# Context keys and values by seven block products: block sums made in DRAM, combined weights beside the first output projection

## The chip, the cores and the metric

The kernel runs on one core of one Trainium2 chip. The metric is device time in microseconds (us) of one execution. Engines are named as in the profile: PE is TensorE (PEld its weight loads), DVE is VectorE, ACT is ScalarE, POOL is GpSimd and SP is SyncE, which here issues DMAs alone.

## What is computed

A post-norm decoder layer on 8 batches of 100 tokens, width 1024, with a context of 8 x 722 tokens. All in float32:

```
x = layernorm(x + retention(x))                 # 8 heads, Wq Wk Wv Wg Wo
x = layernorm(x + cross_attention(x, context))  # 16 query heads, 4 key/value heads of 128
x = layernorm(x + ffn(x))                       # silu(x Wgate) * (x Wup), then Wdown

# cross attention, per batch:
k_ctx = rms_norm(context @ wk_ctx)   # 722 x (4 heads x 128)
v_ctx = context @ wv_ctx             # 722 x (4 heads x 128)
k, v  = own keys (normed, rotated) and own values, joined behind k_ctx, v_ctx
out   = softmax(q k' / sqrt(128) + causal mask) v @ wo
```

The change concerns `k_ctx` and `v_ctx`. For one batch and one key/value head, both are products of a 1024 x 128 weight with the same 722 x 1024 context.

## The kernel before

Activations stand transposed: the feature on the partitions, tokens along the free axis. A float32 operand is kept as two float32r parts, high and low: `split` and `split2` (line 68) make the high part with a copy on ACT and the low part with a subtraction on DVE. `mm3` (lines 90, 93, 94) multiplies high by high, high by low and low by high, so that one block product of 128 features costs three matmuls.

The program is recorded once in Python; a scheduler then orders each engine's instructions by its own estimate of times, and each engine works through its list in that order. A semaphore wait at the head of a list holds everything behind it, on SP's list of DMA issues too.

The stages, in order of time:

- **Retention** (to about 440 us). Heads 1 to 7 use `seven`, which makes a 2 x 2 block product with seven block products for eight. At the end of `core`, once for each of the eight context weights, the weight is split and stored in DRAM (`wcd`), with an accumulating DMA issued by POOL (line 566).
- **First output projection and norm** (`out_proj`, to about 600 us). Weights come through `load_w`: a DMA into one of three staging buffers `wst`, then the split.
- **Cross-attention queries, keys and values of the own tokens** (to about 830 us). Each of 40 projections is followed by a sum over the partitions on POOL (`all_red`, line 141), which the norm on ACT and DVE waits for. The first context batch is loaded and the keys of its first two heads are made here.
- **Context attention** (830 to 1606 us): a loop over 8 batches `b` and 4 key/value heads `kv`. At each batch `load_context` brings in the context of the batch in eight pieces `cs` of 128 x 724 or 128 x 720 and splits each into four `big` tiles. For each head, `context_keys` makes the keys as two column halves of 362 and 360 tokens, 24 matmuls each (`proj`), evacuates them from PSUM (lines 705 to 708) and has POOL sum their squares (line 706, tile `kss`). That sum goes through DRAM (`row`, `rr`) to become a column of scales. `context_values` makes the values in the same way (line 719). Then come the scores (seven chunks, 21 matmuls), a maximum over the partitions on POOL (`mb<-mx`), exponentials, the split of the probabilities into `ph` and `pl`, a sum on POOL (`mb<-sm`) and the product with the values (21 matmuls). The result `oh` goes to DRAM (`o2d`).
- **Second output projection** and the **feed-forward part** with `seven` (1606 us to the end).

Context weights and activations are held so:

- `load_ws` loads one split weight (1 MB) into one of four `w` slots; a head uses two.
- The tiles `big` have four slots, all four used by one batch's context.
- Keys (`kall`) and queries (`q`) have two slots each.

Of the kernel before, what the change touches and what calls it, by code (L numbers as in the profile page):

```python
# [8 lines left out]
F32 = mybir.dt.float32  # L9
# [7 lines left out]
P = 128  # L17
B, T, D = 8, 100, 1024
NB = 4
# [3 lines left out]
SC, SH = 722, 362  # L23
SN = [SH, SC - SH]
# [16 lines left out]
def decoder_layer(ctx, tc, xT, cT, w1, wo1, w2, wo2, wc, w3, wd, gw, qw, kw, trig, dec, mask, out):  # L41
# [44 lines left out]

    pin = tc.keep_in_program_order

# [66 lines left out]

    def tokens_first(pool, acc, copied=True, bufs=1, got=None):
# [17 lines left out]
    o2d = dr.tile([B, P, NKV, 4, 2, T], FR, name="o2d")  # L174
    zd = dr.tile([2, P, KT, N], F32, name="zd")
    zd2 = dr.tile([2, P, KT, N], F32, name="zd2")
    wcd = dr.tile([2 * NKV, P, 2, KT * P], FR, name="wcd")
    hd = dr.tile([QT - 1, 7, P, 2, QT, N], FR, name="hd")
# [35 lines left out]
    kws = cp.tile([P, 1], F32, name="kws")  # L214
# [3 lines left out]
    def load_constants(p, trg):  # L218
# [8 lines left out]
        nc.vector.tensor_scalar(kws, wts[:, 3:4], -0.5 * math.sqrt(P), None, ALU.mult)  # L227
        nc.vector.tensor_scalar(tq, trg[:, 2:4], wts[:, 2:3], None, ALU.mult)
# [9 lines left out]
    def out_proj(half, w, load_o, res, yp, ybufs, p, make_z, dst, z, steps={}, home=None):  # L238
# [7 lines left out]
        for ms in [range(first)] + [[m] for m in range(first, KT)]:  # L246
# [4 lines left out]
            for c in range(2):  # L251
                for m, acc in zip(ms, accs):
                    wt = load_w(w[m, c])
                    for k in range(KT):
# [124 lines left out]

    H = QT * P  # L380
# [96 lines left out]
    with sbuf("l1", 2) as p:  # L477
# [48 lines left out]

        HB = ((0, 0), (1, 1), (0, 1), (1, 0))
# [84 lines left out]
        def after_qk(h, c):  # L612
            for (half, i), acc in c:
                of_qk(half, i, acc)

        def after_v(h, c):
            for (half, blk), acc in c:
                of_v(half, blk, acc, (half, blk) == HB[3])
            core(h)

        def after_g(h, c):
            gated(h, {hb: silu(acc, None if hb == HB[3] else acc) for hb, acc in c})

# [23 lines left out]
    with sbuf("ln1", 1) as p:  # L647
        z1, todo = [], {}
        for half in range(2):
            todo, _ = out_proj(half, wo1, load_o1, xT, p, 2, p, lambda _: [  # L650
                z1p.tile([P, 2, QT, N], FR, tag="z", name="z") for _ in range(2)], zd, z1, todo)
# [13 lines left out]
    kapool = sbuf("ka", 2, "right")  # L665
    ka = kapool.__enter__()
    cz = []
# [21 lines left out]
    def load_context(b):  # L689
        for _ in context_steps(b, wp, 3):  # L690
            pass

    def context_keys(kv):

        kall = ka.tile([P, 2, SC + T], FR, tag="kall", name="kall")
# [17 lines left out]
    def context_values(kv):  # L713

        wv = load_ws(2 * kv + 1)
        vt = ka.tile([P, SC], F32, bufs=1, tag="cvt", name="cvt")
# [12 lines left out]
    with sbuf("l2", 2) as p:  # L729
        ctx0 = context_steps(0, p, 2, behind)  # L730
        for g, group in enumerate(groups):
# [3 lines left out]
            if g in (1, 5):  # L735
                step, kept = context_keys(len(early))
                early.append(kept)
            for half in range(g == 0, 2):
                bs = slice(half * NB, (half + 1) * NB)
                for (kv, i), w in zip(group, ws):  # L740
# [4 lines left out]
                    unit += 1  # L745
                    if i == 5:
# [523 lines left out]
```

## Time and profile before

| | |
|---|---|
| three timed runs | 2483.72, 2486.41, 2486.9 us; median 2486.41 us |
| span of the profiled execution, first to last instruction | 2480.1 us |
| granted TensorE clock | 0.999 |
| PE busy / PEld busy | 2456.9 us / 2436.3 us |
| DVE busy | 1950.7 us |
| ACT busy | 1341.0 us |
| POOL busy | 481.8 us |
| moved by DMA | 433.98 MB, 175 GB/s over the span |

The profile holds one execution. The times of the runs include what lies around the span; for the median that is 6.3 us. An engine's busy time is the union of its instructions. A printed duration runs to an instruction's end, and a next one may start before that end, so sums of durations can exceed the busy time.

### The profile page before, as it was taken

What the parts mean: (1) busy time and instruction counts of PE and PEld (TensorE: products, weight loads), DVE (VectorE), ACT (ScalarE), POOL (GpSimd) and SP (SyncE); (2) the same over time, 40 slices, a digit from 0 to 9 for tenths busy, and PEclk for the clock granted to TensorE, in tenths of its full rate; (3) what the DMA queues carried; (4) which work ended last, traced back from release to release, by engine and by line L of the source; (5) the groups of instructions that cost most, each with busy time, mean ns of one, the idle gap of its engine ahead of it and who ended that gap; (6) DMA issues with size and microseconds to landing.
All of it is one profiled execution on the core that took longest, in us unless ns stands there. A gap on an engine that the chain in (4) does not pass through costs nothing.

```text
span 2480.1 us, 37239 instructions
## 1 busy us (share of the span) xinstructions
PE 2456.9 (99%) x14068; PEld 2436.3 (98%) x14068; DVE 1950.7 (79%) x3101; ACT 1341.0 (54%) x2258; POOL 481.8 (19%) x266
## 2 busy tenths in 40 slices
PE   9999999999999999999999999999999999999997
PEld 9999999999999999999999999999999999999997
DVE  7777877556898798998998999757987777666756
ACT  6667676334888565665566666524544454432221
POOL 0111111100566343443443443100000000000000
PEclk9999999999999999999999999999999999999999
DMA  7333345775544555455455454465455444389731
GB/s 244 112 112 129 132 142 186 242 257 182 173 163 144 196 185 175 130 180 165 154 181 156 155 187 170 156 241 172 160 176 189 161 161 161 122 303 325 265 103 54
DMA packets 221891, 433.98 MB, mean 175 GB/s; under 512 B 47338, under 2 KB 163946, under 8 KB 209294
## 3 DMA queue, kind: packets, MB, share of 16 engines
q1 hardware_dynamic: 217358, 419.49, 50.2%
q0 software_dynamic: 3200, 10.75, 1.9%
q8 instruction: 111, 1.82, 0.3%
q10 hardware_dynamic: 1152, 1.34, 0.2%
q14 instruction: 70, 0.57, 0.1%
HBM read 322.18 MB, written 109.35 MB: 174 GB/s over the span
## 4 chain that ended last, share of the span: by engine, by line
PE 94%; DVE 2%; DMA 2%; ACT 1%; issue 1%; SPq 0%; DVEq 0%; ACTq 0%
PE a L94 20%; PE a L93 20%; PE a L90 20%; PE s L94 9%; PE s L93 9%; PE s L90 9%; PE v L93 2%; PE v L94 2%; PE v L90 2%; PE s L554 1%; PE s L795 1%; PE s L166 1%; DVE y L331 0%; PE v L546 0%; DMA wst<-in_w 0%
## 5 line engine op out<-in xcount | busy, mean ns | idle before, releaser
L90 PE MATMUL a<-big,w 128*128 128x400 f32 (+2 forms) x1808 | 610.7, 339 | 2.0 <-DVE z L270 0.7
L93 PE MATMUL a<-big,w 128*128 128x400 f32 (+2 forms) x1808 | 610.0, 337 | 0.5 <-DVE big L68 0.5
L94 PE MATMUL a<-big,w 128*128 128x400 f32 (+2 forms) x1808 | 608.5, 337 | 0.5 <-DVE w L68 0.5
L68 ACT CAST w<-wst 128x1024 fp32r<-128x1024 f32 (+1 forms) x231 | 239.5, 1039 | 380.3 <-PE s L94 147.6
L68 DVE TENSOR_TENSOR w<-wst,w 128x1024 fp32r<-128x1024 f32 (+1 forms) x231 | 281.1, 1217 | 132.5 <-ACT w L68 130.6
L90 PEld LDWEIGHTS a<-big,w 128*128 128x128 f32 x1808 | 340.2, 188 | 4.5 <-ACT big L68 1.1
L93 PEld LDWEIGHTS a<-big,w 128*128 128x128 f32 x1808 | 340.9, 189 | 2.5 <-DVE big L68 1.3
L94 PEld LDWEIGHTS a<-big,w 128*128 128x128 f32 x1808 | 340.8, 189 | 1.4 <-DVE w L68 0.8
L90 PE MATMUL a<-z,w 128*128 128x400 f32 x680 | 235.0, 346 | 0.4 <-ACT w L68 0.4
L93 PE MATMUL a<-z,w 128*128 128x400 f32 x680 | 235.1, 346 | 0.0
L94 PE MATMUL a<-z,w 128*128 128x400 f32 x680 | 234.9, 346 | 0.0
L90 PE MATMUL s<-big,w 128*128 128x400 f32 x664 | 230.3, 347 | 0.5 <-DMA big<-o2d 0.4
L94 PE MATMUL s<-big,w 128*128 128x400 f32 x664 | 229.2, 346 | 0.4 <-DVE w L68 0.4
L93 PE MATMUL s<-big,w 128*128 128x400 f32 x664 | 229.5, 346 | 0.0
L706 POOL PARTITION_ALL_REDUCE kss<-ksq x64 | 170.2, 2659 | 113.4 <-ACT ksq L705 112.6
L141 POOL PARTITION_ALL_REDUCE ss<-sq x56 | 148.4, 2651 | 199.3 <-ACT sq L750 110.1
L830 ACT ACTIVATE s<-s,rk 128x400 f32<-128x400 f32 x160 | 88.1, 591 | 90.9 <-DVE sm L850 65.3
L90 PEld LDWEIGHTS a<-z,w 128*128 128x128 f32 x680 | 127.8, 188 | 1.2 <-ACT w L68 0.8
L94 PEld LDWEIGHTS a<-z,w 128*128 128x128 f32 x680 | 128.7, 189 | 0.0
L93 PEld LDWEIGHTS a<-z,w 128*128 128x128 f32 x680 | 127.8, 188 | 0.4
L90 PEld LDWEIGHTS s<-big,w 128*128 128x128 f32 x664 | 124.8, 188 | 2.1 <-issue 0.7
L94 PEld LDWEIGHTS s<-big,w 128*128 128x128 f32 x664 | 125.4, 189 | 0.7 <-DVE w L68 0.7
(366 smaller groups left out, 5462.3 us busy)
## 6 DMA issues: line engine op xcount, KB each, us to landing
wst<-in_w SPq DMA_DIRECT2D x135, 512.0 KB
w<-wcd SPq DMA_DIRECT2D x64, 1024.0 KB
wst<-in_wo SPq DMA_DIRECT2D x64, 512.0 KB
hd<-h SPq DMA_DIRECT2D x12, 1400.0 KB
wst<-in_wd SPq DMA_DIRECT2D x64, 256.0 KB
big<-o1d SPq DMA_DIRECT2D x16, 800.0 KB
qd<-d SPq DMA_DIRECT2D x32, 400.0 KB
q<-qd SPq DMA_DIRECT2D x32, 400.0 KB
```

What stands on the lines that cost most here:

```text
L68: return nc.scalar.copy(hi, src), nc.vector.tensor_tensor(lo, src, f32(hi), ALU.subtract)
L90: i = nc.tensor.matmul(acc, lh, rh, start=start, stop=False, skip_group_check=chain)
L93: nc.tensor.matmul(acc, lh, rl, start=False, stop=False, skip_group_check=chain)
L94: nc.tensor.matmul(acc, ll, rh, start=False, stop=stop, skip_group_check=chain)
L141: nc.gpsimd.partition_all_reduce(y, x, P, op)
L166: nc.tensor.transpose(tr[0:T, b * P:(b + 1) * P], vt[:, b * T:(b + 1) * T], ident)
L554: nc.tensor.matmul(bt(o)[:, b], vv[:, b * P:(b + 1) * P], pf[:, b], start=True, stop=True)
L706: nc.gpsimd.partition_all_reduce(ss[:, at], sq[:, at], P, RED.add)
L795: nc.tensor.transpose(tr[0:rows, (c - c0) * P:(c - c0 + 1) * P], vt[:, c * P:c * P + rows], ident)
L830: nc.scalar.activation(sc, sp, AF.Copy, scale=rk[:, c:c + 1])
```

## The change

From the second batch on, keys and values of one head come from one 2 x 2 block product. The context of a batch is cut into four blocks: features 0 to 511 and 512 to 1023, tokens 0 to 361 and 360 to 721 (two tokens are in both). The weights are cut into feature halves: values and keys. Seven block products of 4 x 3 matmuls with 362 columns take the place of eight.

- **Sums of context blocks.** Four for each batch, made in DRAM: `block_sums` copies four blocks into `td` with DMAs issued by SP, and adds to them with four accumulating DMAs issued by POOL. It is a generator, advanced three times per head in the retention stage and then at every third projection of the own queries.
- **Combined weights.** `context_weights` loads both plain context weights of a head, forms four combinations with four DVE operations, splits them (ACT and DVE) and stores them in `wcx`. It is advanced at the weight loads of `out_proj` of the first output projection, from the 13th on.
- **`load_context`** loads and splits seven operands (three blocks as they are, four sums) in 14 pieces of 128 x 724, into the four `big` slots and three new `op` slots.
- **`load_pair`** loads 3.5 MB of weights for a head into the four `w` slots, for 2 MB before.
- **`context_pair`** makes the seven products and puts the keys together in `ks`, the values in `vt`, in SBUF: some parts are copied from PSUM by ACT, others added by DVE. Keys are then scaled, split and squared from `ks`.
- **Room in SBUF.** `kall` has one slot in `ka`, and one more (`ke`) during the first batch; `q` and others in `cx` have one. The score tiles lose the unused part of their first chunk. The pool `y2` of the second output projection opens after the context stage and not before it. `ofs` is dropped, and `oh` is stored with high and low parts apart.

```diff
+    def load_pair(kv):
+        plain = load_ws(2 * kv + 1)
+        ws = [plain[:, :, :H], plain[:, :, H:]]
+        for j, n in ((0, 2), (2, 1), (3, 1)):
+            w = wp.tile([P, 2, 2, H], FR, tag="w", name="w", bufs=4)
+            nc.sync.dma_start(out=f32(w[:, :n]), in_=f32(wcx[kv, :, j:j + n]))
+            ws += [w[:, i] for i in range(n)]
+            if j == 2:
+                nc.sync.dma_start(out=f32(w[:, 1]), in_=f32(wcd[2 * kv, :, :, H:]))
+                ws.append(w[:, 1])
+        return ws
+    def block(b, i, j):
+        return cT[b, :, i * QT:(i + 1) * QT, j * S0:j * S0 + SH]
+    def block_sums():
+        for b in range(1, B):
+            for i, src in enumerate(((0, 0), (1, 1), (0, 0), (1, 0))):
+                pin(nc.sync.dma_start(out=td[b - 1, i], in_=block(b, *src)))
+            yield
+            for i, src in enumerate((block(b, 0, 1), block(b, 0, 1), td[b - 1, 1], td[b - 1, 2])):
+                pin(nc.gpsimd.dma_start(out=td[b - 1, i], in_=src, accum_op=ALU.add))
+                if i > 0:
+                    yield
...
+    def context_weights(pool):
+        for _ in range(12):
+            yield
+        for kv in range(NKV):
+            r0, r1 = (pool.tile([P, KT * P], F32, tag=t, name=t) for t in ("wv", "wk"))
+            nc.sync.dma_start(out=r0, in_=wc[2 * kv + 1])
+            nc.sync.dma_start(out=r1, in_=wc[2 * kv])
...
+            v.tensor_tensor(a22, a22, a21, ALU.subtract)
+            v.tensor_tensor(a21, a11, a21, ALU.subtract)
+            v.scalar_tensor_tensor(a11, a22, -1.0, a11, ALU.mult, ALU.subtract)
+            v.scalar_tensor_tensor(a12, a12, -1.0, a11, ALU.mult, ALU.subtract)
+            for j, srcs in ((0, (a11, a21)), (2, (a22, a12))):
...
+                for n, src in enumerate(srcs):
+                    split2(w[:, n, 0], w[:, n, 1], src)
+                nc.sync.dma_start(out=f32(wcx[kv, :, j:j + 2]), in_=f32(w))
+                for _ in range(2):
+                    yield
...
-    def load_context(b):
-        for _ in context_steps(b, wp, 3):
-            pass
+    def load_context(b, pool):
+        ops = []
+        for src in (block(b, 0, 0), block(b, 1, 0), td[b - 1, 2], td[b - 1, 1], td[b - 1, 0], td[b - 1, 3], block(b, 1, 1)):
+            t = big([P, 2, QT, SH]) if len(ops) < 4 else pool.tile([P, 2, QT, SH], FR, tag="op", name="op", bufs=3)
+            for k in range(0, QT, 2):
...
+                nc.sync.dma_start(out=cs, in_=src[:, k:k + 2])
+                split(t[:, :, k:k + 2], cs)
+            ops.append(t)
+        return ops
...
+    def context_pair(kv, ops, pool):
...
+        def keys(part, scale):
+            nc.scalar.activation(kall[:, 0, part], ks[:, part], AF.Copy, scale=scale)
+            nc.vector.scalar_tensor_tensor(
+                kall[:, 1, part], ks[:, part], scale, f32(kall[:, 0, part]), ALU.mult, ALU.subtract)
+            nc.scalar.activation(ks[:, part], ks[:, part], AF.Square)
+            nc.gpsimd.partition_all_reduce(ss[:, part], ks[:, part], P, RED.add)
+        add = nc.vector.tensor_tensor
+        prod(x, 0)
+        now(nc.scalar.copy, vt[:, lo], x)
+        prod(z, 1)
+        now(add, vt[:, lo], z, vt[:, lo], ALU.add)
+        prod(x, 2, False)
+        now(nc.scalar.copy, ks[:, lo], x)
+        prod(y, 3)
+        now(nc.scalar.copy, ks[:, hi], y[:, at])
+        prod(x, 4, False)
+        now(add, ks[:, hi], x[:, at], ks[:, hi], ALU.add)
+        keys(hi, kwn)
+        prod(y, 5, False)
+        now(add, ks[:, lo], y, ks[:, lo], ALU.add)
+        keys(lo, kws)
+        nc.sync.dma_start(out=row.rearrange("c p -> (c p)")[None, :], in_=ss[0:1])
+        prod(x, 6, False)
+        nc.scalar.activation(vt[:, hi], x[:, at], AF.Copy, scale=-1.0)
+        return (kall, row), vt
```

## The prediction, before the changed kernel was run

> **What bounds the kernel now.** I read the page's busy row first, then the windows by stage, then the groups and waits of the context stage, then timelines of one batch.
>
> ```profile
> PE 2456.9 (99%) x14068; PEld 2436.3 (98%) x14068; DVE 1950.7 (79%) x3101; ACT 1341.0 (54%) x2258; POOL 481.8 (19%) x266
> ```
>
> By this row TensorE is the bound, and work taken from it should be time. The windows (stretch, its length, then busy us of PE, PEld, DVE, ACT, POOL, clock, DMA share, GB/s) say how close the second engine is:
>
> ```profile
> 500.00:640.00 140.00, 140.00 (x776) 137.78 (x775) 91.58 (x141) 63.92 (x103) 12.43 (x13) 1.00 0.64 219
> 640.00:830.00 190.00, 190.00 (x1065) 189.91 (x1065) 165.16 (x301) 148.13 (x294) 109.85 (x47) 1.00 0.51 173
> ...
> 1125.00:1225.00 100.00, 100.00 (x610) 99.30 (x609) 91.76 (x163) 61.37 (x120) 40.25 (x22) 1.00 0.53 162
> 1225.00:1325.00 100.00, 100.00 (x606) 99.41 (x606) 92.97 (x159) 62.67 (x119) 39.40 (x22) 1.00 0.53 169
> ```
>
> In the context stage, where nearly all of the change lies, DVE is busy 92% beside a full PE. The length of a batch there is read off SP's timeline, at the first context load of two batches:
>
> ```profile
> 969.38 1.20 SPq L678 DMA_DIRECT2D cs<-in_cT  x2
> ...
> 1064.42 1.20 SPq L678 DMA_DIRECT2D cs<-in_cT  x2
> ```
>
> A batch takes 95.05 us. Over five batches (1014.5 to 1489.8 us) DVE is busy 438.2 us: 87.6 in a batch, idle 7.4.
>
> **PE, removed.** Per batch and head, 96 projection matmuls become 84. One takes, from start to start in PE's timeline:
>
> ```profile
> 1060.28 0.33 PE L93 MATMUL a<-big,w 128*128 128x362 f32 x1
> ...
> 1067.56 0.33 PE L90 MATMUL a<-big,w 128*128 128x362 f32 x1
> ```
>
> These are 44 matmuls apart, so 0.1655 us each (the printed 0.33 is latency, two run at a time). 12 x 4 heads x 0.1655 = 7.9 us per batch, 55.6 us over the seven batches changed. PE alone would need 95.05 - 7.9 = 87.1 us per batch. If PE stayed the bound, that is the gain, 2.2%.
>
> **DVE, added.** The rows of the context stage (1025 to 1525 us; count | busy, mean ns | idle before):
>
> ```profile
> L68 DVE TENSOR_TENSOR big<-cs,big 128x720 fp32r<-128x720 f32 x20 | 21.2, 1061 | 5.3 <-ACT big L68 5.3
> L68 DVE TENSOR_TENSOR big<-cs,big 128x724 fp32r<-128x724 f32 x20 | 17.5, 894 | 0.0
> L719 DVE COPY cvt<-a 128x360 f32<-128x360 f32 x21 | 10.9, 521 | 0.0
> L708 DVE SCALAR_TENSOR_TENSOR kall<-a,kws,kall 128x362 fp32r<-128x362 f32 x21 | 12.3, 584 | 0.0
> ```
>
> A DVE instruction starts about 0.08 us before the printed end of the one ahead: in DVE's timeline a `vall` of 0.55 us starts at 1031.91 and the next at 1032.38.
> - Operand pieces: 14 splits per batch for 8. Six more at (0.89 + 1.06) / 2 - 0.08 = 0.89 us: 5.3 us.
> - Putting together: three additions per head, less the one copy. The nearest row is that copy, which also reads 360 columns from PSUM: 0.52 - 0.08 = 0.44 us. 2 x 4 x 0.44 = 3.5 us.
> - The two scale-and-subtract operations of the keys stay, at 0.58 us, but now read `ks` in SBUF where they read PSUM. Dropping `ofs` removes no instruction.
>
> Sum: 87.6 + 5.3 + 3.5 = 96.4 us per batch. That is more than PE needs (87.1) and more than the batch takes now (95.05). DVE becomes the bound of the stage, and what PE gives up is not to be had.
>
> **What of DVE's time can change.** Not all of the 87.6 us is work. The same shape with the same kind of operation differs by its company:
>
> ```profile
> L841 DVE TENSOR_TENSOR s<-s,mb 54x216 f32<-54x216 f32 x21 | 19.8, 945 | 1.7 <-POOL mb L141 1.7
> ...
> L853 DVE TENSOR_TENSOR sm<-sm,s 54x216 f32<-54x216 f32 x21 | 7.7, 368 | 0.0
> ```
>
> L841 runs beside POOL's sum for `kss`. Taken over all instructions, what each lasts beyond the shortest of its form adds up to about 12 us per batch, 11.1 of it in instructions that overlap a POOL reduction (7.2 `kss`, 2.8 `mb<-sm`, 1.1 `mb<-mx`). The 16 reductions of a batch all remain. So DVE's bounds are 96.4 - 11.1 = 85.3 us, if none met a reduction any more, and 96.4 + 8 x 0.58 = 101.0, if each of the eight key operations, now reading SBUF alone, is stretched as L841 is (945 - 368 ns). I keep 96.4: the reductions are the same and DVE is busier beside them.
>
> The Trainium skill (SBUF — State Buffer, "Who interferes with whom") states that a DVE instruction with two SBUF inputs contends with a GpSimd instruction that reads SBUF, that one with an input in PSUM does not, and that whoever comes second waits for the whole instruction. This speaks against the change, which moves the source of the key operations from PSUM to SBUF. By that rule each of the eight could wait out a reduction of 2.4 to 2.6 us, about 20 us a batch; the stretches in this trace stay at 1.4 us or less, so the measurement is milder than the rule.
>
> Of DVE's idle 7.4 us, the waits over the five batches put 12.6 (scores, `mx` behind ACT) and 6.4 (`kall` behind ACT) down to things that PE feeds; these go when PE is early. 6.2 + 1.7 us, 1.6 a batch, stand behind POOL's reductions and stay. 96.4 + 1.6 = 98.0 us: 2.95 a batch over today, 20.6 us over seven. Bounds for idle are 0 and today's 7.4.
>
> **What hides the rest.**
> - ACT: six more casts at 0.8 us and three more copies a head at 0.46 us, about 10 us on 58.5 a batch. Covered by 36 us of idle time.
> - DMA in the context stage: 1.5 MB more weights a head and 2.2 MB more context a batch, 15.4 to about 24 MB; the share goes from 0.52 to about 0.8. Covered on average. With single slots each load waits for its slot and holds SP's list: `row`, `rr`, `kall` and `q` stand behind it there, and scores wait for `rr`. I price it at nothing, up to 2 us a batch.
> - First output projection: per head 4 DVE operations and 4 splits of 512 columns. The nearest rows, L430 to L433 of `seven` with the same width, are about 0.7 us: 32 x 0.7 = 22 us on 91.6 of 140, so hidden; without that cover 22 us. Twelve more MB on SP's list, where the stores wait for those splits and the weights of the projection stand behind them. I take 2 us.
> - Block sums: 28 copies and 28 accumulating DMAs of 741 KB. The nearest row for POOL's issue is L566, 128 rows in 0.884 us; four times the rows bound it at 3.5 us. In the retention stage POOL has room; a sum held there waits for units to come. I take 1 us; a burst of four copies ahead of a weight load on SP's list could cost up to 3 us each, 15 in all. Ten of the issues fall into 640 to 830 us, 9 to 35 us on POOL's 110 of 190; behind each stand `ss` sums, for which ACT waits, and PE behind ACT. I take 2 us of 0 to 20.
> - `y2` opening late: the residual loads of the second output projection start after the context stage. 1 us, of 0 to 5.
>
> **Sum.** 20.6 + 2 + 1 + 2 + 1 = about 27 us on the execution's span of 2480.1 us: 2507. The median of the runs shown is 6.3 us above that span: **2513 us**.
>
> **Rivals.**
> 1. *The change works: PE stays ahead.* One mechanism: DVE meets POOL's reductions less often, because its instructions next to them become PSUM reads (the additions). It decides where contention and idle together fall from 12.7 us (11.1 + 1.6) below 9.8 us, since 85.3 + 9.8 = 95.1. At 3 to 8 us of both, a batch takes 88.3 to 93.3: 12 to 47 us gained, 6 lost elsewhere, so 2445 to 2480, 2462 in the middle. For it: PSUM reads such as L708 show no stretch (584 ns). Against it: eight splits in the batch already meet POOL, and there will be 14.
> 2. *Both queues lose.* The next batch's operands have single slots, and 14 splits (12 us of DVE) fall into the last and first head, where PE waits for each. DVE keeps today's 7.4 us idle: 103.8 us per batch, 61 us more, and 6 elsewhere: 2553.
> 3. *A draw.* Contention and idle end at about 10 us: 2486 within 5 us.
>
> **Chances.** DVE-bound and slower 0.6, rival 2 0.15, rival 1 0.18, a draw 0.07. A measurement of this kernel tells about 0.2%, 5 us, from no change. Faster 0.18, the same 0.07, slower 0.75. The range leaves out half of each outer rival: 2462 to 2553. The likeliest case alone holds 2495 to 2535.
>
> **What would show it.** Right: in the context windows DVE at 97% or more, PE at 87 to 90%, PE's largest idle times ended by DVE; a batch of 97 to 100 us at the context loads. Wrong: PE at 98% or more and a batch below 92 us. The key operations above 0.6 us would show the stretch; ACT waiting longer for `ss` between 640 and 830 us the price of the sums.

## The result and the profile after

The changed kernel takes 2717.77 us (median of four runs, 2712.26 to 2721.79) where the kernel before takes 2485.43 us (four runs, 2483.72 to 2486.90). The ratio is 1.0931, with a 95% interval of 1.0914 to 1.0949: slower by 232 us. The forecast was 2513 us, within 2462 to 2553.

The busy row of the page after, and its row of the granted clock, in tenths over 40 slices:

```profile
PE 2490.5 (92%) x13732; PEld 2443.5 (90%) x13732; DVE 2053.8 (76%) x3232; ACT 1410.0 (52%) x2400; POOL 568.5 (21%) x294
PEclk9989898999999999998999999899999999999999
```

PE runs 13732 matmuls for 14068: the 336 that the change removes are gone, 55.6 us by the forecast's 0.1655 us each. But the span of 2713.0 us leaves PE idle for 222.5 us, where before it was 2480.1 - 2456.9 = 23.2 us. And PE is busy longer, not shorter. The granted clock is 0.958, before 0.999. In the trace it is at half for 227 us in 36 stretches, the last of them behind the last matmul. PE is busy in 144 us of them, which costs 72 us. The sum of the span: 199 us more idle time, 72 us lost to the clock, 56 us saved, and 17 us that are not measured by themselves, make the 233 us. (An estimate for most of the 17: PE is interrupted 106 times for 21 before, and each time its last matmul, printed with 0.33 us, outlasts the 0.17 us from one start to the next, 14 us for 85 times.)

The table takes the marks of the stages from the trace: first and last load of the norm's rows `rs`, last store of `qd` or `kd`, every fourth store of `o2d`, first store of `hd`. All in us; "half" is the time at half clock.

| stage | before | after | more | PE idle after | half after | forecast |
|---|---|---|---|---|---|---|
| retention | 439.5 | 517.3 | 77.8 | 69.5 | 68.3 | 1 (0 to 15) |
| first output projection | 124.5 | 136.8 | 12.3 | 5.6 | 6.8 | 2 (0 to 22) |
| own queries, keys, values | 262.0 | 286.8 | 24.8 | 20.6 | 17.1 | 2 (0 to 20) |
| context, first batch | 112.0 | 118.8 | 6.8 | 7.4 | 6.8 | 0 |
| context, seven batches | 667.4 | 768.9 | 101.5 | 102.9 | 112.3 | 20.6 |
| second output projection | 162.0 | 171.9 | 9.9 | 2.5 | 3.8 | 1 (0 to 5) |
| feed-forward | 712.7 | 712.5 | -0.2 | 14.1 | 10.2 | 0 |

Before, PE is idle for at most 2.7 us in any of the first six, and never works at half clock. The idle time of the feed-forward part, 14.3 us before and 14.1 after, lies behind the last matmul but for 1.7 us, and so do its half clocks. Of the 102.9 us, 8.1 end the context stage (1821.1 to 1829.2 us, less than 1 us of it in the next).

The windows after that answer to those shown of before (stretch, length, busy us of PE, PEld, DVE, ACT, POOL, clock, DMA share, GB/s), with one in the retention stage ahead:

```profile
100.00:517.00 417.00, 349.47 (x2029) 343.94 (x2028) 260.83 (x379) 229.71 (x371) 64.50 (x39) 0.92 0.76 175
500.00:640.00 140.00, 134.35 (x744) 132.18 (x743) 88.19 (x122) 60.72 (x85) 13.73 (x17) 0.98 0.91 327
655.00:942.00 287.00, 266.42 (x1450) 261.38 (x1449) 215.65 (x379) 186.51 (x363) 127.33 (x60) 0.97 0.75 203
1100.00:1200.00 100.00, 86.75 (x488) 83.12 (x486) 90.92 (x156) 61.10 (x119) 42.96 (x19) 0.95 0.67 225
1200.00:1300.00 100.00, 90.49 (x481) 88.28 (x482) 88.84 (x156) 61.11 (x118) 37.79 (x18) 0.89 0.59 197
```

In the context stage no engine is full any more: PE 87 and 90, DVE 91 and 89 of 100. A batch takes 105.9 to 115.8 us, 109.8 on average, for 95.1. From one store of `o2d` to the next the four heads of a batch took 23.6, 27.8, 23.9 and 20.0 us before and take 25.9, 37.1, 24.5 and 22.4 us: most of the loss lies where one batch's operands give way to the next one's. The pieces `cs` of one batch were issued within 16 us before (1064.4 to 1080.7) and take 47 after (1070.4 to 1117.6).

**Where PE waits in the context stage.** The waits of PE (1060 to 1829 us: total, times, longest), and some of the largest of ACT and DVE:

```profile
PE a L105 <- DMA w<-wcd: 25.2, 12, 4.0
PE v L108 <- DVE pl L69: 12.8, 10, 2.1
PE v L105 <- ACT ph L69: 12.4, 9, 3.4
PE s L105 <- DMA q<-qd: 10.0, 6, 3.2
PE s L105 <- DVE vall L69: 9.7, 6, 2.2
...
ACT s L992 <- DVE s L986: 53.5, 26, 4.5
ACT rr L947 <- DMA rr<-row: 49.7, 20, 8.5
ACT op L69 <- DMA cs<-td: 31.2, 16, 5.6
...
DVE ksq L809 <- PE a L109: 22.3, 16, 4.3
```

PE waits for weights, which now fill all four slots, and for queries, which have one slot; both come late. It also waits for DVE and ACT, and these wait for PE, for each other, for operands and for the scales. No single wait is long. As I read it, they follow one another around a ring of engines, each of which works through its list in order.

**Where the retention stage waits.** The chain of waits of the kernel after, in order of time, names its longest pieces (start, us, what):

```profile
174.46 30.50 DMA wst<-in_w
...
263.86 22.87 DMA wst<-in_w
...
428.99 3.65 DMA wst<-in_w
435.86 29.25 DMA wst<-in_w
```

A weight load of 512 KB, which landed in 3.65 us at 429, takes 23 to 31 us at three other places. SP's timeline tells what lies ahead of the last of them:

```profile
432.02 3.74 SPq L178 DMA_DIRECT2D td<-in_cT  x4
435.86 34.35 SPq L421 DMA_DIRECT2D wst<-in_w  x3
```

Four copies of 724 KB, issued within 3.7 us, and then the load. Its data come behind theirs: in the trace's packets of SP's queue the rows of the copies (1448 bytes) run from 435.6 to 461.3 us, and the first of the load's (4096 bytes) starts at 458.8. From 444 us on POOL's accumulating DMAs share the DMA engines with them. DVE waits 12.73 us for that load at the combination of weights (line 463), and a subtraction queued behind it on DVE (`tp`, line 457) is what PE waits for: idle from 449.3 to 466.4 us. It is the same at 174 us, by way of ACT. PE's waits of this stage:

```profile
PE a L105 <- ACT w L69: 34.6, 3, 19.4
PE a L105 <- DVE tp L457: 17.1, 1, 17.1
PE s L105 <- ACT sq L590: 11.9, 1, 11.9
```

The third is the other queue: POOL's. Its issues of the sums waited for copies and earlier sums to land, and the sums of the norms were behind them. POOL's rows (count | busy, mean ns | idle before):

```profile
L156 POOL PARTITION_ALL_REDUCE ss<-sq x14 | 40.6, 2902 | 90.0 <-DVE sq L591 90.0
L181 POOL DMA_DIRECT2D td<-in_cT x10 | 12.5, 1433 | 23.7 <-DMA td<-in_cT 23.7
L181 POOL DMA_DIRECT2D td<-td x8 | 9.1, 1142 | 40.2 <-DMA td<-in_cT 31.2 <-DMA td<-td 9.0
```

**The clock.** Windows of two places after, the same columns as above:

```profile
191.00:206.00 15.00, 0.00 (x0) 0.00 (x0) 0.00 (x0) 1.02 (x2) 0.00 (x0) 0.50 1.19 214
206.00:211.00 5.00, 4.93 (x15) 4.88 (x16) 4.84 (x7) 3.26 (x7) 0.00 (x0) 0.50 0.33 130
211.00:216.00 5.00, 5.00 (x29) 5.00 (x28) 3.70 (x7) 3.24 (x6) 3.92 (x2) 1.00 0.00 0
...
1173.60:1177.00 3.40, 3.40 (x14) 3.40 (x13) 2.43 (x4) 1.83 (x4) 0.14 (x1) 0.50 0.05 19
1177.00:1181.00 4.00, 4.00 (x25) 4.00 (x24) 3.35 (x6) 2.73 (x8) 0.94 (x1) 1.00 0.61 128
```

At 206.1 us PE's wait of 19.4 us is over, and for 5 us it makes 15 matmuls where the next 5 us hold 29. In the context stage a wait of 3.3 us (1168.9 to 1172.2) was followed by 3.4 us at half clock. Such stretches came there behind waits, or pairs of waits, of about 2 us and more, in lengths of 3.4, 6.8, 10.2 and 13.7 us.

What decides can be read from the trace. All changes of the clock ahead of the last matmul lie on one grid with steps of 3.413 us: stretches begin at 125.69, 190.55, 279.29 and 361.21 us, 19, 45 and 69 steps behind the first. Each of the 35 stretches at half clock there follows a step in which PE idled for 1.87 us or more; no step at full clock with 1.83 us or less was followed by one. A stretch went on as long as its last step still held about 0.56 us of idle time or more. In the 19 changed kernels together the border is less sharp: it lies between 1.29 and 1.90 us. So what counts is how much idle time falls into one step, and not the length of a single wait: the wait of 2.04 us at 1366.9 lies across the border of two steps, with 1.21 and 0.83 us, and cost no clock.

The Trainium skill (TensorE: Matmul & The Clock Gate, "HAM oscillation — how this bites in real kernels") tells of the same half rate, and asks for no gap above about 3.4 us. In this trace a gap of 1.87 us, at 1584.0, with 0.17 us more in the same step, was enough, while 11 others of 1.0 to 2.0 us stayed without. So the figure is too high for this kernel: most of the waits that cost clock here are 2 to 4 us long.

### The profile page after: what moved, and what is told of

Read it like the earlier page. It is cut to its first block, busy times and chain, and to the rows that moved or that the text cites. A ratio compares the mean times of both kernels' runs of the same rounds, so it can differ in the third digit from the quotient of the medians.

```text
span 2713.0 us, 37298 instructions
## 1 busy us (share of the span) xinstructions
PE 2490.5 (92%) x13732; PEld 2443.5 (90%) x13732; DVE 2053.8 (76%) x3232; ACT 1410.0 (52%) x2400; POOL 568.5 (21%) x294
## 4 chain that ended last, share of the span: by engine, by line
PE 67%; DMA 13%; DVE 10%; issue 4%; ACT 4%; POOL 2%; SPq 0%; DVEq 0%; POOLq 0%; ACTq 0%
PE a L105 14%; PE a L109 14%; PE a L108 14%; PE s L105 7%; PE s L109 7%; PE s L108 7%; DMA wst<-in_w 4%; DMA w<-wcd 2%; PE v L108 1%; PE v L109 1%; PE v L105 1%; DVE s L990 1%; DVE w L69 1%; DMA cs<-td 1%; DMA kd<-d 1%
## 5 line engine op out<-in xcount | busy, mean ns | idle before, releaser
L105 PE MATMUL a<-big,w 128*128 128x400 f32 (+2 forms) x1360 | 481.3, 354 | 108.2 <-ACT w L69 34.6
L108 PE MATMUL a<-big,w 128*128 128x400 f32 (+2 forms) x1360 | 474.0, 349 | 0.2 <-DVE big L69 0.2
L109 PE MATMUL a<-big,w 128*128 128x400 f32 (+2 forms) x1360 | 472.4, 348 | 1.2 <-DVE w L69 1.2
L105 PEld LDWEIGHTS a<-big,w 128*128 128x128 f32 x1360 | 266.0, 196 | 120.1 <-ACT w L69 35.7
L109 PEld LDWEIGHTS a<-big,w 128*128 128x128 f32 x1360 | 266.8, 196 | 2.0 <-DVE w L69 1.8
L108 PEld LDWEIGHTS a<-big,w 128*128 128x128 f32 x1360 | 267.1, 196 | 1.2 <-DVE big L69 0.4
L105 PE MATMUL a<-z,w 128*128 128x400 f32 x680 | 237.9, 350 | 20.6 <-DVE t L166 18.3
L816 POOL PARTITION_ALL_REDUCE kss<-ksq x56 | 194.4, 3513 | 30.6 <-ACT ksq L815 30.6
L105 PEld LDWEIGHTS s<-big,w 128*128 128x128 f32 x664 | 126.5, 191 | 9.1 <-ACT z L69 4.7
L156 POOL PARTITION_ALL_REDUCE mb<-sm x32 | 88.0, 2751 | 207.8 <-DVE sm L995 158.7
## 6 DMA issues: line engine op xcount, KB each, us to landing
wst<-in_w SPq DMA_DIRECT2D x135, 512.0 KB
wst<-in_wo SPq DMA_DIRECT2D x64, 512.0 KB
w<-wcx SPq DMA_DIRECT2D x56, 512.0 KB
```

Of the source, the lines that this page charges most:

```text
L105: i = nc.tensor.matmul(acc, lh, rh, start=start, stop=False, skip_group_check=chain)
L108: nc.tensor.matmul(acc, lh, rl, start=False, stop=False, skip_group_check=chain)
L109: nc.tensor.matmul(acc, ll, rh, start=False, stop=stop, skip_group_check=chain)
L156: nc.gpsimd.partition_all_reduce(y, x, P, op)
L816: nc.gpsimd.partition_all_reduce(ss[:, part], ks[:, part], P, RED.add)
```

## The experiments

Unless said otherwise each time is that of one execution. Runs of the kernel before beside them took 2483.28 to 2489.36 us. How far an edit elsewhere moves a stage can be read from runs that left it as it was. The seven batches of the unchanged context stage took 760.6, 764.0, 768.0, 768.9, 771.7 and 776.8 us, and the unchanged retention stage 512.0 to 522.2 us. So differences below 16 us in the context stage, and below 10 us in the retention stage, are not told apart from that. The stage of e4, 776.8 us, with which f1 to f5 and g1 are compared, is the longest of the six; their mean is 768.3. "Stand-ins" are plain blocks and weights in place of the sums and combinations, so that a run has the loads and not the values.

**e1: no block sums.** The 28 copies and 28 accumulating DMAs are left out, and blocks stand in for sums.

```diff
-                pin(nc.sync.dma_start(out=td[b - 1, i], in_=block(b, *src)))
-                pin(nc.gpsimd.dma_start(out=td[b - 1, i], in_=src, accum_op=ALU.add))
```

> The changed kernel without the block sums: no copies into td, no accumulating DMAs; the four summed operands are loaded from plain context blocks instead, as many bytes in as many pieces, so the keys and values are not those of the reference. Theory A (the sums stall the early stages: POOL's list waits for them, weight loads stand behind their bytes, and the TensorE clock drops to half after each gap): the retention stage is back at its old length, 78 us less, the stage of the own queries 20 to 25 us less, the context stage still 105 to 111 us a batch; about 2620 us. Theory B (the early loss comes from elsewhere, for example from another order of the scheduler): within 30 us of the changed kernel, above 2690 us.

Measured: 2611.22 us. The retention stage is back at 440.7 us and the own queries at 257.6; the context stage stays at 764.0. The sums cost 77 and 29 us in the stages where they are made, and nothing later.

**e2: copies only.**

```diff
-                pin(nc.gpsimd.dma_start(out=td[b - 1, i], in_=src, accum_op=ALU.add))
```

> The changed kernel with the 28 copies into td issued by SP, but without the 28 accumulating DMAs issued by POOL; the sums are therefore plain blocks. Theory A1 (the accumulating DMAs are the larger part: they hold POOL's list until they land and share the DMA engines with weight loads): retention loses 15 to 25 us of its 78, own queries 0 to 5 of 25; about 2640 us. Theory A2 (the copies ahead of the weight loads on SP's list are the larger part): retention keeps 50 us or more of the loss; about 2680 us.

Measured: 2647.3 us; retention 474.8, own queries 267.3. SP's copies alone bring 34 of the 77 us, the accumulating DMAs on top of them 43. The chain of waits has again 21.54, 19.29 and 21.31 us for a load of `wst`. So the copies alone hold the loads back, and a little less than with the sums beside them. A1 holds, with a larger price than it named: the accumulating DMAs are the larger part, and in the own queries too (19 us for 10).

**e3: no combined weights.** They are neither made nor stored; other weights of the same size are loaded in their place.

```diff
-        beside = context_weights(wx)
+        beside = None
```

> The changed kernel without the combined weights beside the first output projection (no loads, no DVE operations, no splits, no stores); the heads load the same number of bytes from the plain split weights, so the result is not the reference's. Theory: the 12 us that the first output projection lost come back, and nothing else moves by more than 5 us; about 2705 us. Rival (the twelve MB of stores and loads also delay what follows): 20 us or more come back.

Measured: 2715.72 us. The first output projection falls from 136.8 to 126.6 us, so the combined weights cost 10 us there. The total hides it: retention (522.2) and own queries (290.5) came out 9 us longer together, within the spread.

**e4: the context stage alone**, e1 and e3 together.

> The changed kernel without the sums and without the combined weights: the seven products alone, with their loads, splits and additions (the operands and weights are plain ones, the result is not the reference's). Theory: the early stages are those of the kernel before, and the context stage keeps its 105 to 111 us a batch by itself; about 2605 us. Rival (the context stage is slow because of something the early stages leave behind, such as late sums or a cold clock): a batch at 96 to 100 us, below 2540 us.

Measured: 2611.01 us; everything ahead of the context stage is as before (439.2, 125.9, 260.4), and the seven batches take 776.8 us. The loss of the context stage is its own. All that follows is built on e4, and its stand-ins are left in, up to i5 but for g2, h1 and h3.

**f1: two weight loads a head** (2 MB, as before; three of the seven products reuse the weights of another), **f2: four operands a batch** (three are used twice), **f3: both.**

```diff
-        ws = [plain[:, :, :H], plain[:, :, H:]]
+        other = load_ws(2 * kv)
+        ws = [plain[:, :, :H], plain[:, :, H:], other[:, :, :H], other[:, :, H:]]
+        ws += [other[:, :, :H], other[:, :, H:], other[:, :, H:]]
...
-        for src in (block(b, 0, 0), block(b, 1, 0), block(b, 0, 0), block(b, 1, 1), block(b, 0, 1), block(b, 1, 0), block(b, 1, 1)):
+        for src in (block(b, 0, 0), block(b, 1, 0), block(b, 0, 0), block(b, 1, 1)):
```

> e4_stage_alone with 2 MB of weights a head for 3.5 MB: two of the four slots, so that the next head's weights load ahead, as in the kernel before; five of the seven products read a part that another one reads too, so the result is not the reference's. Theory W (weights that fill all four slots and cannot load ahead): the waits of PE for w go, about 4 us a batch, with the half-clock stretches behind them another 4, and a batch falls from 111 to 103 us or below; total about 2555 us. Theory D (DVE's work on 14 pieces and the additions): a batch stays at 107 to 111 us; total above 2585 us.

> e4_stage_alone with four operands loaded and split for seven (8 pieces a batch, as before the change); the last three products read the first three operands again, so the result is not the reference's. Theory D: DVE gets 5.3 us a batch less and the burst at the batch's border is gone; a batch falls by 8 to 12 us to about 100; total about 2540 us. Theory W: the waits for w stay and a batch loses 2 to 5 us; total about 2585 us.

> f1 and f2 together: weights, operand pieces and splits of the kernel before, but 84 matmuls a head and the additions. Result not the reference's. If weights and pieces are all that is wrong, PE is the bound again: a batch at 88 to 92 us, total 2455 to 2480 us, faster than the kernel before. If single slots for keys and queries or the order of the seven products matter beside them, a batch stays at 96 us or more, total above 2505 us.

Measured: 2565.35, 2571.22 and 2542.12 us; the seven batches 736.8, 741.7 and 713.2. Against e4 the weights are worth 40 us, the operands 35, both 64; against the mean of the six unchanged stages 8 us less each. f1 and f2 fall between their theories. In f3 PE waits for no weights any more, and yet a batch takes 101.9 us. PE's waits of f3 (1010 to 1550 us):

```profile
PE v L103 <- DVE pl L69: 19.0, 12, 2.0
PE v L100 <- ACT ph L69: 18.0, 9, 2.9
PE a L103 <- DVE big L69: 7.7, 7, 2.0
```

The wait has moved: the product with the values now waits for the softmax.

**f5: no additions on DVE** (copies on ACT in their place, on the base of e4).

```diff
-        now(add, vt[:, lo], z, vt[:, lo], ALU.add)
+        now(nc.scalar.copy, vt[:, lo], z)
```

> e4_stage_alone with the three additions of a head made copies on ACT: 5.3 us a batch less on DVE, as much more on ACT; one part of each sum is left out, so the result is not the reference's. Theory D (DVE's total work sets the batch): a batch falls by 5 us or more, total about 2575 us or less. Theory W or single slots: less than 3 us a batch, total above 2590 us.

Measured: 2580.51 us; the seven batches 752.2, 25 us less than in e4, between the two theories. That is 3.5 us a batch, the 3.5 us that the forecast priced for the additions. Against the mean of the six unchanged stages it is 2.3, so the close agreement is in part chance.

**f4: f3 with two slots for keys and queries**, and `y2` opened ahead of the stage as before. **f6: f4 without additions.**

```diff
-    kapool = sbuf("ka", 1, "right")
+    kapool = sbuf("ka", 2, "right")
-                q = p.tile([P, 4, 2, T], FR, tag="q", name="q")
+                q = p.tile([P, 4, 2, T], FR, tag="q", name="q", bufs=2)
```

> This is f3 (no block sums, no combined weights; two weight loads and four operands a batch, so the products read stand-ins) with two slots again for keys and queries, and the pool y2 open before the context stage as in the kernel before. Theory (single slots and late operands make a chain of waits, PE's idle time and the half clock behind it): the batches fall from f3's 101.9 us to 95 or less, the first batch from 116.7 to about 112, and the second output projection from 172 to 162: together 2542 to about 2480. Rival (the additions and the order of the seven products keep the batch long, slots or not): batches stay at 100 or more, 2525 to 2535 with the second projection's 10 us back. If the second output projection stays at 172, it is the new layout of oh and not the pool.

> f4 with the three additions a head turned into ACT copies as well (sums are left out of keys and values). All that is then left of the change is 84 matmuls for 96 and an order of products. Theory (what holds the batch is latency on DVE and the loads, not the count of products): batches of 88 to 91 us, PE busy 97% or more, clock 0.99, about 2440. Rival (the order of the seven products itself, keys late in a head and their scales behind a trip through DRAM, keeps PE waiting): 95 us or more, PE idle over 5 us a batch, 2480 or more.

Measured: 2531.67 and 2522.58 us; the seven batches 698.4 and 691.8. The rivals of both hold (f4's batches, at 99.8 us, are a little below its 100). The 15 us from f3 to f4 and the 7 from f4 to f6 are within the spread. In f6 all of the additional work is gone, PE has 84 matmuls for 96, and a batch still takes 98.8 us, more than the 95.1 of the kernel before. Opening `y2` early gave nothing back: the second output projection took 174.3 and 175.2 us. By count of matmuls its time is not a loss of its own. Before, 854 fell behind the last store of `o2d`; after and in f4 it is 897: 43 matmuls of it used to run within the context stage.

**g1: the second product made twice**, on the base of e4.

```diff
         prod(z, 1)
+        prod(z, 1, False)
```

> The context stage of the change alone, as e4 (stand-ins for sums and combined weights), with the second product of each head made twice: 12 matmuls more a head, 8.0 us a batch at the full clock, 56 us in all. The matmuls of the kernel before are then back in number. Theory (PE's work is not on the path, it waits for late operands and runs at half clock behind each wait): the time stays within 15 us of e4's 2611, and PE's idle time falls by some 30 to 60 us. Rival (PE's work is on the path between the waits): 2611 + 56 = 2667 or more.

Measured: 2624.97 us, 14 us more than e4 for 56 us of matmuls. PE's idle time fell from 138.6 to 116.7 us, by less than the 30 to 60 us expected; the time at half clock fell from 136.9 to 94.3. So 56 us of matmuls cost 14 us here: where PE waits and slows anyway, most of what the change takes from it was never to be had.

**g2: no sums of sums**, on the full change.

```diff
-            for i, src in enumerate((block(b, 0, 1), block(b, 0, 1), td[b - 1, 1], td[b - 1, 2])):
+            for i, src in enumerate((block(b, 0, 1), block(b, 0, 1), block(b, 1, 1), block(b, 0, 0))):
```

> The full change, but the two accumulating DMAs that read an earlier sum read a context block instead: same count and bytes, no wait of POOL for a landed sum (two of the four sums a batch are then other sums). Theory (POOL's queue, held by the wait for landings of 10 to 20 us, delays the sums of the norms and with them PE): the retention stage falls from 517 us to 480 to 490, own queries from 287 to 270 to 275, POOL's waits for td from 55 us to under 10. Rival (the load of the DRAM-to-DRAM transfers on the DMA engines does it, late weights before all): retention stays at 505 or more. The context stage stays at 769 within 8 in both.

Measured: 2703.63 us; retention 509.6, own queries 279.5. In the retention stage the rival holds: PE's wait of 11.9 us behind POOL is gone, those behind late weights stay (41.1 and 18.1 us). The edit takes away the waits for landed sums, worth 8 us at most in each stage; POOL still waits 38.1 us for copies in the retention stage (64.0 in the full change), but none of PE's larger waits there is behind it. So there the load on the DMA queues is the larger part. In the own queries, 279.5 us lie above the theory's 270 to 275, and both paths show. The chain of waits of the kernel after has these pieces (start, us, what), followed by ACT's wait for the sums of the norms (655 to 942 us):

```profile
759.12 22.52 DMA kd<-d
...
825.10 13.79 DMA td<-in_cT
...
840.12 5.66 POOL ss L156 x2
...
ACT s L143 <- POOL ss L156: 29.0, 18, 7.6
```

The store of `kd` is ahead of PE's wait at 778.8 us (5.1 us); the copy, which POOL waits for, and then the two sums are ahead of its longest, 8.5 us at 844.3. ACT's wait is 21.7 us in g2, but 7.6 in e2, which has the copies alone, and 7.8 before.

**f7, f8: a second slot for `ks`** in f6 and in f4. In f6 PE's largest wait (1010 to 1550 us) was for the copy of new keys into `ks`, which waited for POOL's sum of the keys before:

```profile
PE a L100 <- ACT ksq L801: 15.7, 4, 4.7
```

> f6 with a second slot for ks, the tile in which keys are put together, then squared, and read by the sum over the partitions on POOL. In f6 PE still waited 15.7 us of 540 for the ACT copy of new keys into ks, which waited for POOL. Theory (the single slot of ks is a chain PE, ACT, POOL, ACT, PE that the kernel before did not have): the seven batches fall from 691.8 us to 640 to 665, PE's wait on that copy to under 3 us, 2470 to 2497 in all. Rival (the order of the seven products and the softmax behind them, v waiting for ph and pl, is what is left): 680 or more, 2512 or more, and the waits of v for ph and pl grow.

> f4 with a second slot for ks, additions kept. Theory of the single ks slot: the seven batches fall from 698.4 us to 665 to 680, 2500 to 2515 in all. Rival (softmax and DVE): 690 or more, 2524 or more.

Measured: 2539.85 and 2558.16 us, 17 and 26 us more than without the slot. That wait did go (3.8 us in f7), but others came: 17.7 us for casts of operands on ACT in f7. My theory of the single `ks` fell. Its rival has the times, but not its sign: the waits of `v` for `ph` and `pl`, 6.4 and 9.4 us in f6, did not grow (3.7 and below 2.8 in f7).

**h1, h3: the same in the full change**, nothing left out. h1 gives `ks` two slots and `vt` one; h3 puts keys, squares and their sum into one tile with two slots.

```diff
-        ks = ka.tile([P, SC], F32, tag="ksq", name="ksq", bufs=1)
+        ks = ka.tile([P, 6 * P], F32, tag="kss", name="ks", bufs=2)
-        ss = ka.tile([P, 6 * P], F32, tag="kss", name="kss", bufs=1)
+        ss = ks
```

> The full change, nothing left out, with two slots for ks and, to make room, one for the values vt. Theory of the single ks slot: 5 to 25 us less than 2718 in the context stage, if the late operands do not hide it. Rival (late weights and operands set the batch in the full change): within 5 us of 769 in the context stage, or more if the single slot of vt makes a wait of its own.

> The full change, nothing left out: keys, squares and the sum over the partitions share one tile with two slots, vt keeps its two. Same expectation as for h1 without the price of a single vt: 2693 to 2713 by the theory of the single ks slot, 2713 to 2723 by the rival.

Measured: 2736.51 and 2695.86 us. h3 gains 22 us on the median of the change, 15 of them in the context stage (753.7, 7 below the shortest unchanged one). That is within the theory's 2693 to 2713, in one run, against f7 and f8. The single `vt` of h1 costs more than its slot brings (793.1). h3 is still 206 us behind the kernel before.

**i4: every product in a fresh PSUM bank**, on the base of f6; **i5: i4 with two slots for `ks` and for the scores.**

```diff
-        prod(x, 2, False)
+        x = bank("a")[:, :SH]
+        prod(x, 2)
```

> f6 with every product begun in the next of the three PSUM banks instead of added onto the bank that a copy has just read (sums of products are left out as well), and y2 opened after the stage again. In f6 and in the full change the copy out of a bank must be done before the product two further on may be added to it: five turnarounds PE, ACT or DVE, PE in a head, each covered by one product of 2.0 us, of a kind the kernel before has not. Theory (these turnarounds are what is left of the loss): the seven batches fall from f6's 691.8 us to 640 to 665, PE's idle time from 54.6 to under 25. Rival (the softmax of one head after the other, its single tile s, and the splits of the next operands on DVE at the turn of the batch set the pace): 680 or more, with the maximum's sums on POOL still 21 to 23 us apart in a batch and 27 to 35 across two batches.

> i4 with two slots for ks and two for the scores s. Theory of turnarounds and single slots together: PE near its floor of 87.1 us a batch, 610 to 635 for the seven, 2430 to 2450 in all. Rival (what is left lies in the order of the in-order lists, planned by estimates of time that the chip does not keep, and moves with every edit): 660 or more.

Measured: 2494.32 and 2586.39 us; the seven batches 671.0 and 760.0. i4 falls between the two forecasts: against f6 the turnarounds through a bank that has just been read are worth 21 us, little more than the spread, and 95.9 us a batch are left, with PE idle for 43 us. The Trainium skill (Perfetto Trace Analysis, "Matmuls") says that independent groups of matmuls should change banks so that evacuation lies beside the next group. The seven products are not independent, and I take these 21 us for a price of that.

i5 is the surprise: more room, 89 us slower. Waits of PE and ACT in i5 (1010 to 1500 us):

```profile
PE a L100 <- ACT ksq L802: 24.4, 9, 7.8
...
ACT rr L946 <- DMA rr<-row: 56.2, 13, 10.3
ACT vall L69 <- PE v L103: 38.1, 25, 4.3
ACT ksq L802 <- POOL kss L809: 30.5, 6, 8.2
```

PE's largest wait is for the copy of new keys, which waits for POOL's sum, as in f6, although `ks` has two slots. ACT's waits for `v` and for POOL's `kss` are not among its larger ones in i4: its list now has the next head's `vall` and keys ahead of other work. That the scheduler plans further ahead with more slots, by estimates that the chip does not keep, is my reading; no run shows it by itself.

## Why the forecast was wrong

The direction was right, the size was not: 27 us forecast, 233 measured. Of the 206 us between them, 81 lie in the seven context batches, 100 in the two stages where the block sums are made (77 and 23), 10 in the first and 9 in the second output projection, 7 in the first context batch.

**Right.** PE's removed matmuls (55.6 us by count). DVE's work: 96.4 us a batch forecast, about 97 measured in the seven batches. The additions: a duration of 0.52 us forecast, 0.53 measured. The bytes: 24 MB a batch forecast, 164.9 MB over seven measured. The key operations did stretch where they meet POOL's sums, but only among those with 362 columns, where about half took 1.18 us (after, 1060 to 1829 us):

```profile
L813 DVE SCALAR_TENSOR_TENSOR kall<-ksq,kwt,kall 128x362 fp32r<-128x362 f32 x26 | 22.2, 853 | 0.0
L813 DVE SCALAR_TENSOR_TENSOR kall<-ksq,kwt,kall 128x360 fp32r<-128x360 f32 x26 | 15.2, 585 | 1.1 <-ACT kall L812 1.1
```

That is 0.27 us on four of the eight, about 1 us a batch, far from the 20 us of the rule that the forecast weighed and below its bound of 101.0. Of the forecast's signs, PE at 87% came, but this confirms nothing: DVE, which was to be at 97% or more and to end PE's largest waits, is at 88%, and the largest are for weights.

**The step that failed first: idle time beside DVE.** The forecast said of DVE's waits for PE "these go when PE is early" and left 1.6 us a batch. Its sum has a gap there as well: the rows that it names come to 5.4 of the 7.4 us, and the other 2.0 were dropped without a reason. About 1 us of them is a wait that depends on loads and not on PE (before, 1014.5 to 1489.8 us):

```profile
DVE big L68 <- ACT big L68: 5.3, 5, 1.8
```

After, DVE is idle for 109.8 - 97, about 13 us a batch, by the row of the seven batches:

```profile
1060.00:1828.60 768.60, 665.70 (x3642) 643.23 (x3640) 678.12 (x1136) 462.78 (x880) 313.47 (x137) 0.93 0.64 214
```

A bound by one engine holds if the others run ahead of it, and none does here: PE waits for DVE and ACT, these wait for PE and for loads. The sum of DVE's work set a floor, not the time. Of rival 2, which let PE wait for operands and DVE keep its idle time, the mechanism was there; its 103.8 us a batch were too few.

**Loads in the context stage**, "I price it at nothing, up to 2 us a batch". f3 gives back 63.6 us in seven batches, 9.1 a batch, for weights and operands; some 5 of it are the six splits a batch that f3 saves on DVE, by the forecast's price. "Covered on average" was true, the DMA share is about 0.6. But loads wait for a slot that comes free late, and PE stands by: 25.2 us for weights and 10.0 for queries.

**The clock**, which the forecast did not price at all: 72 us in the whole run, 48 of them in the seven batches. A wait of about 2 us within one step of the grid costs its length and about half of the 3.4 us or more that follow.

**Block sums**, 1 us in the retention stage and 2 in the own queries, measured 78 and 25. The bound of 15 us came from SP's issue: "a burst of four copies ahead of a weight load on SP's list could cost up to 3 us each". What counts is when the data of the load behind them land: 23 to 31 us for 3.65. e2 shows that the copies alone hold the loads for 19 to 22 us, and that the accumulating DMAs add the larger part of the time in both stages. In the retention stage POOL's held queue, the price that the forecast looked at, is the smaller part of it (g2). In the own queries the forecast's path, ACT waiting longer for `ss`, did come, with 29.0 us for 7.8; there the size was wrong, and late stores came beside it.

**Combined weights**, 2 us forecast, 10 to 12 measured, within the bound of 22. **`y2`**, 1 us forecast: in f4, with the early opening, that stage is no shorter (174.3 us); the 10 us of the second output projection are mostly its matmuls that used to fill the end of the context stage.

**What stays open.** With weights, operands, slots, additions and turnarounds given back (i4) the context stage takes 671.0 us, no less than the 667.4 of the kernel before with 12 matmuls a head more. PE still waits there, 12.0 us in 490 for copies of values on ACT and 9.2 for `v` behind `pl`, and I take it that the softmax of one head after the other and the order of the lists hold it; no run shows that alone. f7, f8 and i5 show that an edit which only adds room can move the stage by 16 to 89 us. So the worth of single covers, measured one after another, is not exact, and whether another order would let the 55.6 us out was not tried.

## What to carry to other kernels

Where a second engine is over 90% busy beside the full one, work taken from the full one need not be time: add up the turnarounds between them, and look at what the removed work was covering. A transfer's price to others is when the data of the loads queued behind it land, not how long its issue takes. Price a gap on PE with the clock that follows it: here about 1.7 us more where 1.9 us or more of one step of 3.413 us are idle.

## What the runs showed of the hardware

- Half clock comes in whole steps of a grid of 3.413 us, up to 20.5 us around a wait of 19.4 us. In the trace of the kernel after, each stretch ahead of the last matmul follows a step with 1.87 us or more of idle PE, and none a step with 1.83 us or less.
- Bursts of four copies of 724 KB within DRAM hold a load of 512 KB issued behind them for 23 to 31 us, with accumulating DMAs under way beside them, and for 19 to 22 us without (e2). Accumulating DMAs of 724 KB landed after 19.5 us (adding a block of the context) and 9.5 us (adding an earlier sum), medians in the retention stage, where the accumulating DMA of 512 KB into `wcd` takes 7.3. POOL's own part of an issue is 1.0 to 1.2 us in the median.
- Contention between DVE and POOL goes both ways. The sum of the squares of the keys on POOL (`kss`) took 2.46 us in the median and 5.04 at most before; after it is 2.59 and 11.55, by a profile whose times on POOL are rough. In these rows (count | busy, mean ns | idle before; the kernel before from 1010 to 1490 us, then the kernel after from 1060 to 1829 us) its mean goes up by a third:

```profile
L706 POOL PARTITION_ALL_REDUCE kss<-ksq x41 | 107.2, 2615 | 67.9 <-ACT ksq L705 67.3
```

```profile
L816 POOL PARTITION_ALL_REDUCE kss<-ksq x54 | 187.2, 3508 | 30.6 <-ACT ksq L815 30.6
```

Sums of 4.8 and 4.9 us, twice the shortest, lie beside a row of DVE subtractions that read two operands from SBUF (`s<-s,mb`, at 1144 and 1168 us, say). The forecast looked at what such a meeting costs DVE and not at what it costs POOL, whose sum the scales of the keys wait for.
